# One-column products for carried sums, an ordering edge for node steps, and half runs as row groups in a four-layer graph network

## The chip, the cores and the metric

The kernel runs on one core of a Trainium2 chip. The metric is the device time of one execution in microseconds (us). A core has five engines that run side by side, each with an instruction queue of its own that is worked off in order: TensorE (PE, matrix products; its weight loads are listed as PEld), VectorE (DVE), ScalarE (ACT), GpSimd (POOL, here it issues the indirect transfers) and SyncE (SP, here it issues the plain transfers). TensorE reads SBUF and writes PSUM; the other engines move results on.

## The reference

A residual network of four graph layers over N = 6250 nodes and E = 100000 edges, sorted by destination. Before each layer the node state x (160 columns: 64 scalars, 32 vectors) is normalised and cut at zero to h. A layer mixes h with weights, takes each edge's source row, multiplies it by weights that a small network computes from the edge's features, and adds the edge messages up by node. Layer 3, cut to what matters:

```python
h = jax.nn.silu(edge_scalars @ fc_w1 * (1.0 / np.sqrt(8.0)))
weight = h @ fc_w2 * (1.0 / np.sqrt(64.0))
gs = f_s[edge_src]
gv = f_v[edge_src]
m0a = gs * ys * w1_
m0b = jnp.sum(gv * yv[:, None, :], -1) * INV3 * w4_
m1a = gs[..., None] * yv[:, None, :] * w2_[..., None]
m1b = gv * ys[..., None] * w3_[..., None]
mid = jax.ops.segment_sum(edge_feat, edge_dst, num_segments=N)
```

Layers 0 and 1 have the same form. Layer 2 reads the state at an edge's destination and sums by source:

```python
xs = s[dst]
xv = v[dst]
agg = jax.ops.segment_sum(tp, src, num_segments=N) / DENOM
```

## The kernel before

The edges, sorted by destination, are cut into 56 windows (NW) of 14 tiles (WT) of 128 edges. A window is made of two half runs of 896 consecutive edges; the tiles of the two half runs alternate. A pair of windows is a unit u, and its 28 tiles are worked in 7 groups of G = 4 tiles, so each layer has 28 x 7 = 196 groups.

The program runs in stages. The prologue makes tables of positions and layer 0's node inputs. Then `edges(0)`, `edges(1)`, `messages2`, `sums2` and `edges(3)` follow.

**`edges(li)`**, for layers 0, 1 and 3. Its loop over groups asks for a group's source rows six groups ahead (`gather`: four indirect transfers on POOL, L1277, into `ge`, eight buffers), computes the edge network (`hidden`, L1266 or L1260 with ACT's L1269; `edge_weights`, L1300 or L1293, scaled by ACT into `ws`, L1304 and L1306), and forms the messages on VectorE (`messages`: the selector `oh` L1319, then L1330, L1331, L1333, L1336, L1337, L1338). Four products L1394 add the messages up into `pg`: edges of the first half run land in rows 0 to 63, of the second in rows 64 to 127, each by its node's distance from the first node of its half run.

At a window's end ACT copies `pg` to `acc` (L1397) and a generator `nodes` starts. It takes two steps per group, behind the group's products, in `nodes_out` and `nodes_in`: four products with `turn` (a 0/1 matrix of 128 x 128, L1346) transpose the sums and put the two halves together by node (L1062, into `pt`); ACT copies them to `at` (L1069); VectorE adds the sum of the node that the window before shares with this one: column 0 of that window's `at` to column 1 of this one's (L1073); PE multiplies by the output weights (L1080, L1082); VectorE adds the result to the state `xt` (L1095, L1096, in layer 3 L1115 and on). For layers 0 and 1 the normalisation of the new state and the next layer's node products follow (L991 and on, L999, L1009, L1010, L1022), and SP writes the next layer's `table`, `skip` and `x` (L1034, L1047, L1048). In layers 0 and 1 every third group also takes a step of a generator that sorts the edges by source for layer 2; these are VectorE steps (L1166, L1168, L1171, L1172).

**`messages2`** makes layer 2's messages. For each window SP loads 128 rows of the node table, from the window's first node on (`tb`, L1443), and the destinations of all its 1792 edges, the same to every partition (`dt`, L1445). VectorE compares them with each partition's node (`oh`, L1447). Four products per group (L1479) pick each edge's row, ACT copies the result (L1484 to L1486), VectorE forms the message in `row` (L1497 to L1506, five buffers), and POOL writes each tile's 128 rows to their place by source (L1509).

**`sums2`** reads these rows back in order and sums them on PE (L1611, L1613), with transposes in place of `turn`.

A scheduler in the tile framework orders the instructions on each engine by priority and dependencies. Buffers come from pools; an instruction that reuses one waits for its last reader.

Of the kernel before, what the change touches and what calls it, by code (L numbers as in the profile page):

```python
# [11 lines left out]
F32 = mybir.dt.float32  # L12
# [677 lines left out]
class Fast:  # L690
# [16 lines left out]
    def prologue(self):  # L707
# [119 lines left out]
        nc.tensor.matmul(pw[:, 2, :], lhsT=self.ones[0:1, :], rhs=wd[:, 3, :], start=True, stop=True)  # L827
        nc.vector.tensor_scalar(self.plus_w, pw[:, 0, :], iota_p, None, op0=ALU.add)

        column = pro.tile([P, NW], F32, name="column0")  # L830
        nc.vector.tensor_scalar(column, pw[:, 1, :], place, None, op0=ALU.add)
        other = pro.tile([P, NW], F32, name="other")
        nc.vector.tensor_tensor(other, column, pw[:, 2, :], ALU.not_equal)
# [217 lines left out]
    def nodes_out(self, li, xt, sk, acc, turn, carry, w, wk, pp):  # L1051
# [5 lines left out]
        for k in range(4):  # L1057
            rows, o = (96, 3 * MV) if k == 0 else (MV, (k - 1) * MV)
            if turn is None:
                nc.tensor.transpose(pt[:rows, k, :], acc[:, o : o + rows], self.ident[:n, :n])  # L1060
            else:
                nc.tensor.matmul(pt[:rows, k, :], lhsT=acc[:, o : o + rows], rhs=turn, start=True, stop=True)  # L1062
        yield
# [4 lines left out]
        else:  # L1068
            nc.scalar.copy(at, pt)  # L1069
        if turn is not None:  # L1070

            if carry[0] is not None:
                nc.vector.tensor_add(at[:, :, 1], at[:, :, 1], carry[0][:, :, 0])  # L1073
            carry[0] = at
        yield
# [123 lines left out]

    def at(self, k, most=N):  # L1200

        return self.nc.values_load(self.first[0:1, 2 * k : 2 * k + 1], engines=[mybir.EngineType.SP], min_val=0, max_val=most,
                                   skip_runtime_bounds_check_because="a node's number")

    def edges(self, li):
# [103 lines left out]
        def messages(u, g):  # L1309
# [27 lines left out]
            tt(mvec[:, :, :, 0:64], by3(t1, 64), yv[:, :, :, None].to_broadcast([P, n, 3, 64]), ALU.mult)  # L1337
            tt(mvec[:, :, :, 64:96], e1, by3(ws[:, :, 64:96], 32), ALU.mult)  # L1338
            return oh, msg

        carry = [None]

        def nodes(k, acc):
            xt, sk = xts.pop(k)
            turn = nk.tile([P, P], F32, name="turn")
            nc.vector.tensor_scalar(turn, self.iota, self.column[:, k : k + 1], None, op0=ALU.is_equal)  # L1346
# [35 lines left out]
        for i, (u, g) in enumerate(groups):  # L1382
            prepare(i + AHEAD)
            weights_of(i + 2)
            if i + 1 < len(groups):
                edge_weights(*groups[i + 1])
            oh, msg = messages(u, g)
            for k in range(width(u, g)):
                t = 2 * WT * u + G * g + k
                end = t % WT == WT - 1 or t == TT - 1  # L1390
                if t % WT == 0:
                    pg = p_g.tile([P, AW], F32, name="pg")
                half = slice(HN * (t % 2), HN * (t % 2) + HN)
                nc.tensor.matmul(pg[half], lhsT=oh[:, k, :], rhs=msg[:, k, :AW], start=t % WT < 2, stop=t % WT >= WT - 2)  # L1394
                if end:
                    acc = wk.tile([P, AW], F32, name="acc")
                    nc.scalar.copy(acc, pg)  # L1397
                    live.append(nodes(t // WT, acc))
            data.pop(u - 1, None)
            live = [n for n in live if not (next(n, True) or next(n, True))]  # L1400
            if li < 2 and i % 3 == 0:
# [9 lines left out]
    def messages2(self):  # L1411
# [26 lines left out]
        def select(k):  # L1438

            n = min(WT, TT - WT * k) * P  # L1440
            at = self.at(k)
            tb = ld.tile([P, 160], F32, name="tb")
            nc.sync.dma_start(tb, self.table[2][ds(at, P), :])  # L1443
            dt = ld.tile([P, WT * P], I32, name="dt", bufs=2)
            nc.sync.dma_start(dt[:, :n], self.a["dst_w"][k : k + 1, :n].to_broadcast([P, n]))  # L1445
            oh = ld.tile([P, WT, P], F32, name="oh", bufs=3)
            nc.vector.tensor_scalar(oh.rearrange("p t e -> p (t e)")[:, :n], dt[:, :n], self.plus_w[:, k : k + 1], None,  # L1447
                                    op0=ALU.is_equal)
# [23 lines left out]
        def messages(u, g):  # L1472
            n = width(u, g)
            t0 = 2 * WT * u + G * g
            ts = slice(t0, t0 + n)
            pe = p_e.tile([P, G, 256], F32, name="pe")
            for k in range(n):
                tb, oh = ohs[(t0 + k) // WT]
                nc.tensor.matmul(pe[:, k, :160], lhsT=oh[:, (t0 + k) % WT, :], rhs=tb, start=True, stop=True)  # L1479
            pw = pws.pop((u, g))[:, :n]  # L1480
            pe = pe[:, :n]
            row = wk.tile([P, G, RW], F32, name="row", bufs=5)[:, :n]
            ev = wk.tile([P, G, 224], F32, name="ev", bufs=3)[:, :n]
            nc.scalar.copy(ev[:, :, 0:160], pe[:, :, 0:160])  # L1484
            nc.scalar.copy(ev[:, :, 160:224], pe[:, :, 64:128])
            nc.scalar.copy(row[:, :, 294:390], pe[:, :, 64:160])  # L1486
            nc.scalar.copy(row[:, :, 256:262], self.edge_in[:, ts, :])
# [165 lines left out]
def _layout(inputs):  # L1653
# [46 lines left out]
    a["dst_t"] = by_tile(i["dst"], 1 << 20).T  # L1700
    a["dst_w"] = by_tile(i["dst"], 1 << 20).reshape(NW, WT * P)
    rec0 = np.zeros((E, 8), np.float32)
# [58 lines left out]
```

## Time and profile before

| | us |
|---|---|
| median of three runs | 5459.54 |
| lowest and highest | 5449.31, 5473.62 |
| the profiled execution | 5448.67 |
| its span, first to last instruction | 5446.9 |

The profile is one execution of the program. Its stages, by the first and last indirect transfer of each: prologue to 171 us; layer 0's gathers 171 to 1265; layer 1's 1324 to 2395; layer 2's scatters 2455 to 3550; its sums to 4380; layer 3's gathers 4380 to 5420. A row of the groups reads: line, engine, operation, output and inputs by their names in the program, how many; then the busy time, the mean duration of one in ns, and the idle time of the engine just before them with what ended most of it. Some rows that the change touches:

```profile
L1479 PE MATMUL pe<-tb,oh 128*128 128x160 f32 x1568 | 348.4, 363 | 112.5 <-ACT row L1486 112.3
...
L1062 PE MATMUL pt_out<-turn,acc 128*96 128x128 f32 x1344 | 212.6, 309 | 0.6 <-ACT acc L1397 0.6
...
L1447 DVE TENSOR_SCALAR oh<-dt,plus_w 128x1792 f32<-128x1792 int32 x56 | 65.6, 1171 | 15.8 <-DMA dt<-in_dst_w_dram 15.7
...
L1073 DVE TENSOR_TENSOR at<-at 96x4 f32<-96x4 f32 x165 | 26.7, 162 | 191.6 <-ACT at L1069 190.4
```

A product of f32 operands stands in the trace as two passes: 784 products of L1479 are 1568 rows.

### The profile page before, as it was taken

The numbers are of one execution on the slowest core, as the hardware profiler recorded it, in microseconds if no ns is written. First come the engines' busy times: TensorE is split into PE (matmuls) and PEld (weight loads), VectorE is DVE, ScalarE is ACT, GpSimd is POOL, SyncE is SP. The second block draws the span as 40 slices with busy tenths as digits, with TensorE's granted clock in tenths as the row PEclk, the third lists the DMA queues.
The fourth block names the chain that finished last, engine by engine and source line by source line (L and its number), as shares of the span: only waits on it lengthen the run. The fifth ranks groups of instructions, "written<-read, shape, count | busy, mean of one in ns | idle before, by whom it ended". The sixth has DMA issues, their size and how long they took to land.

```text
span 5446.9 us, 77043 instructions
## 1 busy us (share of the span) xinstructions
PE 4624.0 (85%) x22084; PEld 2866.7 (53%) x22084; DVE 4217.8 (77%) x11655; ACT 2087.1 (38%) x6858; POOL 3346.0 (61%) x3143
## 2 busy tenths in 40 slices
PE   6799999997999999976666666689999988888887
PEld 4455555554555555544444444478888844444443
DVE  6688889888878897867777777767777767777777
ACT  5344444443544444533333333312222243343433
POOL 0577777774777777747777777700000067777776
PEclk9899999998989898987787877799999978788887
DMA  3333333322333333336666666477777533333332
GB/s 95 105 97 88 91 87 90 88 75 73 98 94 94 90 95 93 90 101 239 215 219 215 222 218 223 166 283 237 238 235 237 164 87 80 82 81 82 83 79 57
DMA packets 371211, 733.89 MB, mean 135 GB/s; under 512 B 69677, under 2 KB 249098, under 8 KB 370650
## 3 DMA queue, kind: packets, MB, share of 16 engines
q1 hardware_dynamic: 207122, 379.11, 22.3%
q0 software_dynamic: 163072, 349.43, 22.0%
q8 instruction: 180, 2.95, 0.2%
q14 instruction: 253, 2.07, 0.1%
q10 hardware_dynamic: 584, 0.33, 0.0%
HBM read 519.59 MB, written 209.08 MB: 134 GB/s over the span
## 4 chain that ended last, share of the span: by engine, by line
PE 52%; DVE 16%; DMA 14%; POOL 6%; issue 5%; ACT 3%; SPq 0%; DVEq 0%; ACTq 0%; POOLq 0%
PE pg L1394 12%; PE pg L1613 7%; DMA rec<-row,edge_to 7%; PE pw L1300 7%; DMA ge<-table,rt 6%; PE pg L1611 5%; POOL ge L1277 5%; PE ph L1266 4%; PE pa L1022 3%; PE pt_out L1062 2%; PE po L1082 2%; POOL rec L1509 2%; PE ph L1455 2%; DVE msg L1337 2%; PE pw L1293 2%
## 5 line engine op out<-in xcount | busy, mean ns | idle before, releaser
L1277 POOL DMA_INDIRECT ge<-table,rt x2352 | 2489.1, 1058 | 1774.1 <-DMA skip<-sk 830.3
L1394 PE MATMUL pg<-msg,oh 128*64 128x384 f32 x4704 | 1061.4, 572 | 165.6 <-DVE msg L1338 139.7
L1509 POOL DMA_INDIRECT rec<-row,edge_to x784 | 856.1, 1092 | 299.0 <-issue 191.2
L1304 ACT ACTIVATE ws<-pw,rt 128x96 f32<-128x96 f32 x2352 | 695.8, 348 | 820.5 <-DVE msg L1338 298.6
L1300 PE MATMUL pw<-w_w2y,hh 100*128 100x192 f32 x3136 | 673.5, 353 | 10.6 <-ACT ws L1306 7.7
L1394 PEld LDWEIGHTS pg<-msg,oh 128*64 128x64 f32 x4704 | 305.9, 150 | 709.0 <-issue 252.5
L1300 PEld LDWEIGHTS pw<-w_w2y,hh 100*128 100x128 f32 x3136 | 534.9, 202 | 236.9 <-ACT ws L1306 138.6
L1337 DVE TENSOR_TENSOR msg<-msg,yls 128x768 f32<-128x768 f32 x588 | 555.7, 945 | 0.0
L1613 PE MATMUL pg<-msg,oh 128*120 128x288 f32 x1668 | 541.5, 406 | 0.0
L1330 DVE TENSOR_TENSOR pr<-ge,yls 128x384 f32<-128x384 f32 x588 | 320.2, 545 | 220.7 <-DMA ge<-table,rt 219.9
L1269 ACT ACTIVATE hh<-ph 100x1024 f32<-100x1024 f32 (+1 forms) x336 | 269.1, 801 | 463.7 <-PE pw L1293 206.2
L1479 PE MATMUL pe<-tb,oh 128*128 128x160 f32 x1568 | 348.4, 363 | 112.5 <-ACT row L1486 112.3
L1266 PE MATMUL ph<-ft,w_w1r 12*100 12x512 f32 (+1 forms) x784 | 382.3, 658 | 71.2 <-ACT hh L1269 57.0
L1611 PE MATMUL pg<-rt,oh 128*120 128x192 f32 x1668 | 410.0, 328 | 29.3 <-DMA rt<-rec 29.3
L1479 PEld LDWEIGHTS pe<-tb,oh 128*128 128x128 f32 x1568 | 277.6, 226 | 274.5 <-ACT row L1486 221.9
L1333 DVE TENSOR_TENSOR msg<-ws,ge 128x512 f32<-128x512 f32 x588 | 402.0, 684 | 0.0
L1306 ACT COPY ws<-pw 128x192 f32<-128x192 f32 x1176 | 388.5, 330 | 0.0
L1455 PE MATMUL ph<-ft,w_w1d 128*128 128x512 f32 x224 | 162.4, 819 | 263.2 <-ACT hh L1457 262.4
L1502 DVE TENSOR_TENSOR row<-pw,ev 128x512 f32<-128x512 f32 x196 | 135.2, 690 | 301.8 <-ACT row L1488 298.3
L1611 PEld LDWEIGHTS pg<-rt,oh 128*120 128x120 f32 x1668 | 298.0, 184 | 117.6 <-issue 30.7
L1331 DVE TENSOR_REDUCE dot<-pr 128x128 f32<-128x384 f32 x588 | 344.2, 585 | 0.1
L1338 DVE TENSOR_TENSOR msg<-ge,ws 128x384 f32<-128x384 f32 x588 | 324.4, 552 | 0.0
(486 smaller groups left out, 7327.6 us busy)
## 6 DMA issues: line engine op xcount, KB each, us to landing
rt<-rec SPq DMA_DIRECT2D x208, 780.0 KB
dt<-in_dst_w_dram SPq DMA_DIRECT2D x56, 896.0 KB
ge<-table,rt POOLq DMA_INDIRECT x2352
ft<-in_ft_dram SPq DMA_DIRECT2D x56, 512.0 KB
ft<-in_ft_dram SPq DMA_DIRECT2D x28, 896.0 KB
xt<-x SPq DMA_DIRECT2D x168, 82.0 KB
rec<-row,edge_to POOLq DMA_INDIRECT x784
rt<-in_rec_dram SPq DMA_DIRECT2D x84, 112.0 KB
```

What stands on the lines that cost most here:

```text
L1266: nc.tensor.matmul(ph[:, i], lhsT=w1[r : r + K, :], rhs=ft[r : r + K, 4 * P * (j // 2) :][:, : 4 * P], start=True, stop=True)
L1277: nc.gpsimd.indirect_dma_start(out=ge[:, k, :], out_offset=None, in_=self.table[li], in_offset=bass.IndirectOffsetOnAxis(ap=rt[:, G * g + ...
L1300: nc.tensor.matmul(pw[:, i, :192], lhsT=hh[:, k + i, :], rhs=w2, start=True, stop=True)
L1304: nc.scalar.activation(ws[:, k0 + i, 0:96], pw[:, i, 0:96], AF.Copy, scale=rt[:, G * g + k0 + i, 0:1])
L1306: nc.scalar.copy(ws[:, k0 : k0 + m, 96:192], pw[:, :m, 96:192])
L1333: tt(msg[:, :, AW - 64 : AW + 64].rearrange("p g (k u) -> p g k u", k=2), ws.rearrange("p g (k u) -> p g k u", k=2)[:, :, :, 0:64], e0[:, ...
L1337: tt(mvec[:, :, :, 0:64], by3(t1, 64), yv[:, :, :, None].to_broadcast([P, n, 3, 64]), ALU.mult)
L1394: nc.tensor.matmul(pg[half], lhsT=oh[:, k, :], rhs=msg[:, k, :AW], start=t % WT < 2, stop=t % WT >= WT - 2)
L1479: nc.tensor.matmul(pe[:, k, :160], lhsT=oh[:, (t0 + k) % WT, :], rhs=tb, start=True, stop=True)
L1509: d = nc.gpsimd.indirect_dma_start(out=self.rec2, out_offset=bass.IndirectOffsetOnAxis(ap=self.edge_to[:, t0 + k : t0 + k + 1], axis=0), i ...
L1611: nc.tensor.matmul(pg[:, 0:192], lhsT=oh[:, k, :], rhs=rt[:, k, 0:192], start=first, stop=end, skip_group_check=True)
L1613: nc.tensor.matmul(pg[:, 192:480], lhsT=oh[:, k, :], rhs=msg[:, k, :], start=False, stop=end, skip_group_check=True)
```

## The change

In `nodes_out` VectorE's add of the carried column goes. Instead, behind each of the four products with `turn`, TensorE adds a product with one column: the window before's `acc` times the column 0 of its `turn`, added into column 1 of `pt`. For this `carry` keeps the window before's `acc` and `turn`, and both get four buffers in place of two.

In `edges` the steps of the node generators are traced inside a block that ties VectorE's instructions among them behind the group's last message instruction.

In `messages2` each half run has its own table rows and destinations: partitions 0 to 63 hold the 64 table rows from the first half run's first node on and its 896 destinations, partitions 64 to 127 those of the second. A product contracts the 64 rows of its tile's half run, and the results of the first half run lie in the first bank of `pe`, those of the second in the other; ACT's copies read them in the order of the tiles. `plus_w` and the array `dst_w` are laid out for it.

```diff
-        nc.vector.tensor_scalar(self.plus_w, pw[:, 0, :], iota_p, None, op0=ALU.add)
...
+        nc.vector.scalar_tensor_tensor(self.plus_w, column, -1.0, pw[:, 0, :], op0=ALU.add, op1=ALU.add)
...
-            else:
-                nc.tensor.matmul(pt[:rows, k, :], lhsT=acc[:, o : o + rows], rhs=turn, start=True, stop=True)
+                continue
+            nc.tensor.matmul(pt[:rows, k, :], lhsT=acc[:, o : o + rows], rhs=turn, start=True, stop=carry[0] is None,
+                             skip_group_check=True)
+            if carry[0] is not None:
+
+                sums, turned = carry[0]
+                nc.tensor.matmul(pt[:rows, k, 1:2], lhsT=sums[:, o : o + rows], rhs=turned[:, 0:1], start=False,
+                                 stop=True, skip_group_check=True)
+        if turn is not None:
+            carry[0] = acc, turn
         yield
...
-        if turn is not None:
-
-            if carry[0] is not None:
-                nc.vector.tensor_add(at[:, :, 1], at[:, :, 1], carry[0][:, :, 0])
-            carry[0] = at
...
-            tt(mvec[:, :, :, 64:96], e1, by3(ws[:, :, 64:96], 32), ALU.mult)
-            return oh, msg
+            last = tt(mvec[:, :, :, 64:96], e1, by3(ws[:, :, 64:96], 32), ALU.mult)
+            return oh, msg, last
...
-            turn = nk.tile([P, P], F32, name="turn")
+            turn = nk.tile([P, P], F32, name="turn", bufs=4)
...
-                    acc = wk.tile([P, AW], F32, name="acc")
+                    acc = wk.tile([P, AW], F32, name="acc", bufs=4)
...
-            live = [n for n in live if not (next(n, True) or next(n, True))]
+            with tc.issue_after(last.ins):
+                live = [n for n in live if not (next(n, True) or next(n, True))]
...
-            n = min(WT, TT - WT * k) * P
-            at = self.at(k)
             tb = ld.tile([P, 160], F32, name="tb")
-            nc.sync.dma_start(tb, self.table[2][ds(at, P), :])
-            dt = ld.tile([P, WT * P], I32, name="dt", bufs=2)
-            nc.sync.dma_start(dt[:, :n], self.a["dst_w"][k : k + 1, :n].to_broadcast([P, n]))
-            oh = ld.tile([P, WT, P], F32, name="oh", bufs=3)
-            nc.vector.tensor_scalar(oh.rearrange("p t e -> p (t e)")[:, :n], dt[:, :n], self.plus_w[:, k : k + 1], None,
+            dt = ld.tile([P, WT // 2 * P], I32, name="dt", bufs=2)
+            for h in range(2):
+                rows = slice(HN * h, HN * h + HN)
+                nc.sync.dma_start(tb[rows], self.table[2][ds(self.at(k, half=h), HN), :])
+                nc.sync.dma_start(dt[rows], self.a["dst_w"][2 * k + h : 2 * k + h + 1, :].to_broadcast([HN, WT // 2 * P]))
+            oh = ld.tile([P, WT // 2, P], F32, name="oh", bufs=3)
+            nc.vector.tensor_scalar(oh.rearrange("p t e -> p (t e)"), dt, self.plus_w[:, k : k + 1], None,
                                     op0=ALU.is_equal)
...
-                nc.tensor.matmul(pe[:, k, :160], lhsT=oh[:, (t0 + k) % WT, :], rhs=tb, start=True, stop=True)
+                h, rows = k % 2, slice(HN * (k % 2), HN * (k % 2) + HN)
+                nc.tensor.matmul(pe[:, 2 * h + k // 2, :160], lhsT=oh[rows, (t0 + k) % WT // 2, :], rhs=tb[rows],
+                                 start=True, stop=True)
+            pe = pe.rearrange("p (h t) c -> p t h c", h=2)
+            pair = lambda v: v.rearrange("p (t h) c -> p t h c", h=2)
...
-            nc.scalar.copy(ev[:, :, 0:160], pe[:, :, 0:160])
-            nc.scalar.copy(ev[:, :, 160:224], pe[:, :, 64:128])
-            nc.scalar.copy(row[:, :, 294:390], pe[:, :, 64:160])
+            nc.scalar.copy(pair(ev[:, :, 0:160]), pe[:, :, :, 0:160])
+            nc.scalar.copy(pair(ev[:, :, 160:224]), pe[:, :, :, 64:128])
+            nc.scalar.copy(pair(row[:, :, 294:390]), pe[:, :, :, 64:160])
...
-    a["dst_w"] = by_tile(i["dst"], 1 << 20).reshape(NW, WT * P)
+    a["dst_w"] = np.append(i["dst"], np.full(TT * P - E, 1 << 20, np.int32)).reshape(2 * NW, WT // 2 * P)
```

## The prediction

> **What bounds the kernel now.** I read the page first (engine shares, the 40 slices, the costliest groups), then one table of busy time by stage, then the timeline of POOL, then the waits of each stage, last the chain of waits inside layer 0. The page:
>
> ```profile
> PE 4624.0 (85%) x22084; PEld 2866.7 (53%) x22084; DVE 4217.8 (77%) x11655; ACT 2087.1 (38%) x6858; POOL 3346.0 (61%) x3143
> ...
> POOL 0577777774777777747777777700000067777776
> ...
> L1277 POOL DMA_INDIRECT ge<-table,rt x2352 | 2489.1, 1058 | 1774.1 <-DMA skip<-sk 830.3 <-issue 581.9 <-DVE w_osr L898 170.0
> L1509 POOL DMA_INDIRECT rec<-row,edge_to x784 | 856.1, 1092 | 299.0 <-issue 191.2 <-ACT ev L1485 62.1 <-DVE row L1502 14.6
> ```
>
> POOL looks 61% busy and harmless. But its idle time is a start (170), the stage of layer 2's sums (830), two stage borders (58 and 60), and "issue". The table by stage, in the order layer 0, layer 1, layer 2's messages, its sums, layer 3 (columns: us, busy of PE, PEld, DVE, ACT, POOL, PE clock, DMA share, GB/s):
>
> ```profile
> 171.00:1324.00 1153.00, 1080.18 (x5154) 620.86 (x5154) 1005.81 (x2746) 530.10 (x1650) 855.60 (x785) 0.91 0.34 89
> 1324.00:2455.00 1131.00, 1033.37 (x4768) 568.79 (x4768) 913.09 (x2613) 516.36 (x1732) 832.50 (x785) 0.90 0.36 95
> 2455.00:3550.00 1095.00, 699.30 (x3302) 470.03 (x3302) 778.18 (x1610) 373.32 (x1076) 855.85 (x784) 0.79 0.61 214
> 3550.00:4380.00 830.00, 809.37 (x4292) 680.59 (x4292) 602.45 (x1795) 178.00 (x691) 0.08 (x1) 0.98 0.70 228
> 4380.00:5447.00 1067.00, 890.63 (x4255) 455.67 (x4254) 814.57 (x2403) 406.38 (x1456) 801.20 (x784) 0.83 0.31 79
> ```
>
> The timeline of POOL in layer 2's messages, and VectorE's selector there:
>
> ```profile
> 2824.74 0.97 POOL L1509 DMA_INDIRECT rec<-row,edge_to  x1 [0.30 <-issue]
> ...
> 2826.02 1.68 POOL L1509 DMA_INDIRECT rec<-row,edge_to  x1 [0.30 <-DVE pr L1500]
> ...
> 2826.43 1.15 DVE L1447 TENSOR_SCALAR oh<-dt,plus_w 128x1792 f32<-128x1792 int32 x1
> ...
> 2828.01 1.35 POOL L1509 DMA_INDIRECT rec<-row,edge_to  x1 [0.30 <-issue]
> ```
>
> Every indirect transfer is followed by 0.30 us and the next one, through all four edge stages. 784 of them at the median 0.946 + 0.305 us are 981 us; layers 0, 1 and 3 spend 1094, 1071 and 1040 us from first to last gather, and the rest is transfers that last longer than 0.946. Layer 2's scatters: 784 x (0.972 + 0.305) = 1001 of 1095 us. So POOL, not PE, is what these stages wait for, and no faster compute engine shortens layers 1, 3 or layer 2's messages by itself. VectorE's waits agree (before the first product of a group, for layers 1 and 3):
>
> ```profile
> DVE pr L1330 <- DMA ge<-table,rt: 65.6, 55, 3.7
> ...
> DVE pr L1330 <- DMA ge<-table,rt: 144.1, 70, 6.4
> ```
>
> Layer 0 is different: there that wait is 10.2 us in all, and the last gather is issued at 1265.3 us while the last message ends at 1287.9: the compute side ends some 22 us late (8 us in layer 1: 2394.8 and 2403.2). The chain inside layer 0 (230 to 1262 us):
>
> ```profile
> by line: PE pg L1394 25.5%; PE pw L1300 22.0%; PE ph L1266 13.6%; PE pa L1022 8.6%; PE pt_out L1062 5.0%; ACT hh L1269 3.4%; PE po L1082 2.9%; issue 2.0%; DVE msg L1337 1.7%; PE po L1080 1.3%; POOL ge L1277 1.2%; PE pt_in L1009 1.2%; DVE ms
> ```
>
> Some 80% of it is PE. Layer 0 is the one edge stage where PE is the limit, by a little.
>
> **What the Trainium skill says.** "SBUF — State Buffer", section "SBUF: two separate sides": a transfer issued by GpSimd has its descriptors written by GpSimd's cores, and while VectorE runs an instruction in a two-port mode GpSimd is locked out of SBUF until it ends; an instruction with two SBUF inputs takes the same port. The trace agrees: the two scatters beside L1447 above last 1.68 and 1.35 us instead of 0.97. "TensorEngine Tiling (Array Packing)", "Instruction Overhead": a product with one column costs as much as one with some 60. No run here shows it yet. "TensorE: Matmul & The Clock Gate", "What's actually happening": activity opens the clock, idleness halves it; the table agrees (0.98 in the sums, 0.79 in layer 2's messages), so more PE work will not cost clock, and I put the clock at no change.
>
> **The change part by part.**
> (a) *VectorE's add of the carried column (L1073) goes.* 165 adds x 0.162 = 26.7 us busy, and the 190.4 us that VectorE waited before them for ACT (41.3 in layer 0, 92.4 in layer 1, 56.8 in layer 3). Layers 1 and 3 are POOL's: worth nothing there, the wait moves to the gathers or to the next step, L1095/L1115, which needs the product L1082. In layer 0 some of the 41 comes back, because PE waits for messages.
> (b) *Its replacement on PE:* four one-column products per window, 165 windows with a predecessor, so 660 products; the trace lists each f32 product as two passes, so 1320, and 440 per layer. Price: the existing eight passes of L1062 start at 711.28 and the next product at 712.25, at most 0.12 us each; their 128 columns fill that. A one-column pass is bound by loading 96 weight columns, an estimate of 0.08 us (that TensorE page, "LDWEIGHTS": columns / 1.2). Bounds 0.08 and 0.108, so 35 to 48 us per layer. In layers 1 and 3 it lies beside POOL; PE idles 8% of layer 1 (1033 busy of 1131), so I add 2 us there, up to 15 if that slack can't be used. In layer 0 it stands on the chain: up to +40. Against it stand the 41.3 us under (a), the 9 us that PE idled before L1080 for that add, and what PE waited for messages. I take +8, bounds -18 (the whole lag of 22 us but a rest of 4 goes) and +40.
> (c) *Node steps behind the messages.* In the instruction order of the two built programs VectorE's queue is the same apart from the missing adds: of some 11,000 instructions about 30 change the group they stand in, and PE and ACT shift by a fraction of a group. The new ordering edge pins what stood there already: 0. The third and fourth buffers of acc and turn only keep a window's sums alive for the next: 0.
> (d) *Half runs in layer 2's messages.* The broadcast of destinations shrinks from 128 x 1792 to 2 x 64 x 896 words per window, 917 to 459 KB, 56 times: 51 to 26 MB of the stage's 234 (214 GB/s x 1095 us). Transfers are not what POOL waits for (its waits there are 0.3 us each): 0 in the steady state. The products L1479 contract 64 rows, two of them side by side: PE is 64% busy here, 0. ACT's three copies only read in another order: ACT is busy 373 of 1095 us and waits 482 us for free rows, 0. SP issues four transfers and two register loads per window instead of two and one; 112 more transfers in 1095 us, asked for one window ahead, hidden; if not, the selector would come late, and its slack is a window's 20 us. What counts is L1447: 1.17 to about 0.6 us, 56 times. Over all rows of that stage, 86 of 784 scatters overlap an L1447 and are 0.371 us above 0.97 on average, the other 698 are 0.091 above: 86 x 0.28 = 24 us is its doing. Half as long it meets fewer scatters and holds each a shorter time: a third to a half of the cost is left, a gain of 16 (bounds 8 and 24).
> (e) *Border layer 1 to layer 2:* 60 us, on whose chain the first broadcast (8.8 us) and the write of the last x behind it (12.3 us) stand. With a quarter of the bytes at first, -7 (0 to -13). The prologue swaps one VectorE step for another: 0. The end of layer 3 trades add and wait, about 0.3 us, for eight slow passes: +1.
>
> Sum: +8 +2 -16 -7 +1 = -12 us. The profiled execution took 5448.67 us (span 5446.9), so 5437; the median of the runs shown, 5459.54, is 0.2% above it, and there the sum gives about 5447. I put 5445.
>
> **Rivals.**
> *Faster:* VectorE's waits at nodes were what kept layer 0 behind POOL. Then the lag goes (-18), the selector gives its full 24, the border 10, layer 1 nothing: -50, 5410. For it: in layer 0 VectorE's idle time lies almost wholly at node steps. Against: those waits are for PE, which is late itself.
> *Slower:* the one-column products decide in PE's queue. Layer 0 +40, and layer 1, whose PE load becomes that of layer 0 today, ends 15 us late; less 16 and 7: +32, 5492. It decides from the point where PE's passes per group pass POOL's 5.6 us. For it: pt_out stands on layer 0's chain with all of its time (5.0%; 54 x 0.97 us of these 1032 is 5.1%). Against: PE has idled for the add.
> *The change does nothing on the device's limit:* only the selector counts, -16 to -23 with layer 0 at 0: it is inside the main case.
>
> **How the numbers follow.** Half a per cent (27 us) is about what a measurement of this kernel tells from no change. Main case 45%, own range 5425 to 5465: a third of it is faster by over 0.5%, two thirds within. Faster rival 27%, all faster. Slower rival 28%: 23 slower, 5 within. Sums: faster 0.42, same 0.35, slower 0.23. The range 5392 to 5502 holds both rivals with the spread of the runs (0.2%).
>
> **What would show it.** The gaps of POOL stay 0.30 us in all four stages; the mean scatter falls from 1.092 to about 1.07 us; L1447's successor near 0.6 us; 1320 more passes of 0.08 to 0.11 us; L1073 gone and its wait found before L1095 and the gathers. The lag at layer 0's end tells the rivals apart: 22 us unchanged (main), about 4 (faster), 35 or more with POOL blocked by full buffers (slower). I would be wrong altogether if gathers themselves got shorter or longer in layers 1 and 3, where nothing of this touches them.

## The result and the profile after

The changed kernel takes 5526.66 us (median of 4 runs, 5522.12 to 5552.52), the kernel before in the same series 5466.58 us. The ratio is 1.0126, with a 95% interval of 1.0089 to 1.0163: it is 1.3% slower, and the interval doesn't reach 1. The forecast was 5445, its range ended at 5502. The profiled execution took 5530.79 us (span 5529.0). It lies 82 us above the profiled execution of before, the medians only 60 apart: that execution of before, at 5448.67 us, is among the shortest of its kernel.

The page of the changed kernel, in the lines that answer to those of before:

```profile
PE 4679.0 (85%) x23404; PEld 2969.0 (54%) x23404; DVE 4168.4 (75%) x11490; ACT 2082.5 (38%) x6858; POOL 3299.5 (60%) x3143
...
POOL 0577677775577777773777777720000057777775
...
L1280 POOL DMA_INDIRECT ge<-table,rt x2352 | 2477.0, 1053 | 1880.7 <-DMA skip<-sk 829.8
...
L1517 POOL DMA_INDIRECT rec<-row,edge_to x784 | 821.8, 1048 | 316.7 <-issue 184.0
```

POOL is less busy than before (3299.5 us against 3346.0): its transfers got shorter, the scatters above all (1048 ns on average against 1092). But it sat idle 107 us longer ahead of the gathers (1880.7 against 1774.1). The same five stages by busy time (us, busy of PE, PEld, DVE, ACT, POOL, PE clock, DMA share, GB/s), cut where POOL goes on to the next stage:

```profile
171.00:1413.00 1242.00, 1166.51 (x5594) 693.00 (x5594) 1002.76 (x2697) 532.74 (x1650) 846.52 (x784) 0.88 0.32 83
1413.00:2570.00 1157.00, 1066.23 (x5220) 611.38 (x5220) 902.04 (x2562) 517.39 (x1735) 831.79 (x784) 0.90 0.35 92
2570.00:3630.00 1060.00, 613.75 (x3290) 416.78 (x3290) 752.32 (x1604) 365.24 (x1072) 821.29 (x784) 0.71 0.58 198
3630.00:4460.00 830.00, 808.64 (x4292) 680.40 (x4292) 600.81 (x1791) 176.41 (x690) 0.51 (x1) 0.98 0.70 228
4460.00:5529.00 1069.00, 912.82 (x4695) 496.66 (x4694) 807.30 (x2351) 407.68 (x1457) 798.66 (x784) 0.84 0.31 79
```

Layer 0 takes 1242 us instead of 1153 (+89), layer 1 1157 instead of 1131 (+26), layer 2's messages 1060 instead of 1095 (-35); its sums and layer 3 are as they were. In layers 0 and 1 PE is busy 86 and 33 us longer. What POOL waited for in layer 0 (us in total, times, longest):

```profile
POOL ge L1280 <- issue: 194.8, 639, 0.4
...
POOL ge L1280 <- DVE bst L991: 45.0, 11, 8.8
POOL ge L1280 <- DVE msg L1341: 20.4, 5, 6.8
POOL ge L1280 <- DVE xt L1041: 14.7, 6, 6.0
```

The "issue" row is the 0.30 us between transfers that was there before. The long gaps in the others are new: 32 gaps over 0.35 us, 90 us together. POOL stands until VectorE has done with a gather buffer: 31 of the 32 end 0.27 us after the last read (L1341) of the group eight before, and there are eight buffers. (The rows name whatever VectorE instruction ended nearby.) In the second half of layer 0 of the kernel before, the first VectorE product of a group's messages (L1330) began some 22 us after its last gather. Now it is some 33 us, mostly 30 to 42 (L1333), and there the gather buffers are all taken.

In POOL's own terms this is the whole of layer 0's 89 us: 81 us of gaps beyond 0.30 us each, a border to layer 1 that is 17.5 us longer (75.9 against 58.4), less 9 us of shorter transfers. VectorE's waits in layer 0, before and after:

```profile
DVE at L1073 <- ACT at L1069: 41.3, 24, 3.3
DVE xt L1095 <- PE po L1082: 27.8, 37, 4.8
```

```profile
DVE xt L1098 <- PE po L1085: 130.8, 55, 7.5
DVE xt L1041 <- ACT tb L1033: 67.2, 17, 8.1
DVE hk L1004 <- ACT hn L999: 27.0, 13, 5.7
```

L1098 is the L1095 of before. Its wait for `po` was 27.8 us, with 41.3 us of waiting ahead of the add that is now gone: 69 us have become 131. In layer 1 the same two waits, 116 us together, have become 176.

A stage's length can be split by the clock record of its trace: the time lost to a lowered TensorE clock (length x (1 - granted clock), summed piece by piece), and the rest, the length at full clock. It is an account and not a cause: where a stage doesn't wait for TensorE, a lowered clock need not cost anything (the half runs below are such a case). Each layer with the border behind it, in us, from one execution of each kernel, the experiments below included (A and B mark kernels that ran side by side in one series):

| kernel | layer 0: length | full clock | lost | layer 1: length | full clock | lost |
|---|---|---|---|---|---|---|
| before | 1152.3 | 1052.6 | 99.8 | 1131.0 | 1012.3 | 118.7 |
| changed | 1241.5 | 1089.3 | 152.2 | 1157.1 | 1037.7 | 119.5 |
| one-column products alone (A) | 1229.6 | 1081.0 | 148.6 | 1184.6 | 1041.4 | 143.2 |
| order edge and half runs (A) | 1187.8 | 1056.5 | 131.3 | 1136.9 | 1013.9 | 123.0 |
| changed, update one step later (A) | 1197.2 | 1081.5 | 115.8 | 1152.4 | 1036.1 | 116.3 |
| half runs alone (B) | 1161.6 | 1052.6 | 109.0 | 1133.4 | 1010.3 | 123.1 |
| order edge alone (B) | 1175.3 | 1056.0 | 119.3 | 1136.7 | 1013.7 | 123.0 |
| changed, one-column products twice | 1252.1 | 1135.3 | 116.8 | 1210.9 | 1068.3 | 142.6 |
| half runs, add and update one step later (B) | 1165.5 | 1063.0 | 102.5 | 1123.3 | 1019.3 | 104.0 |

At full clock the passes show plainly: +36.7 us in layer 0 and +25.4 in layer 1 for the change. The other 52.4 us of layer 0 are lost clock, and nearly all of it fell while TensorE was busy (93.3 us lost in busy time before, 145.9 after).

How much clock is lost differs from one execution to the next. But every execution has its span and mean clock on record, so the split can be made for whole kernels over all executions (medians, us):

| kernel | executions | full clock | lost |
|---|---|---|---|
| before (A) | 37 | 4809 | 663 |
| one-column products alone (A) | 4 | 4880 | 695 |
| order edge and half runs (A) | 20 | 4710 | 741 |
| changed, update one step later (A) | 18 | 4764 | 714 |
| changed | 4 | 4759 | 768 |
| changed, one-column products twice | 4 | 4845 | 782 |
| before (B) | 13 | 4812 | 649 |
| order edge alone (B) | 9 | 4818 | 658 |
| half runs alone (B) | 5 | 4689 | 738 |

Rows without a letter are from series of their own. The products alone cost some 70 us at full clock and 32 us of lost clock. (Among the executions of the two kernels the lengths at full clock don't overlap; the lost clock does.) The half runs show why lost clock is no cost by itself: they lose 89 us more of it and are shorter all the same. In the profiled executions 80 us of this lie in layer 2's messages (228.1 before, 308.5 us), where POOL is the limit.

### The profile page after: what moved, and what is told of

Same layout as the page of the kernel before. It is cut to its first block, busy times and chain, and to the rows that moved or that the text cites. A ratio compares the mean times of both kernels' runs of the same rounds, so it can differ in the third digit from the quotient of the medians.

```text
span 5529.0 us, 79941 instructions
## 1 busy us (share of the span) xinstructions
PE 4679.0 (85%) x23404; PEld 2969.0 (54%) x23404; DVE 4168.4 (75%) x11490; ACT 2082.5 (38%) x6858; POOL 3299.5 (60%) x3143
## 4 chain that ended last, share of the span: by engine, by line
PE 25%; DMA 8%; DVE 8%; POOL 6%; issue 4%; ACT 2%; SPq 0%; DVEq 0%; ACTq 0%; POOLq 0%
PE pg L1621 7%; DMA rec<-row,edge_to 6%; PE pg L1619 5%; POOL rec L1517 4%; PE pg L1397 4%; POOL ge L1280 2%; DMA ge<-table,rt 2%; PE pw L1296 2%; PE po L1085 1%; DVE row L1510 1%; PE ph L1263 1%; PE pt_out L1062 1%; PE pa L1022 1%; PE ph L1459 1%; DVE msg L1340 1%
## 5 line engine op out<-in xcount | busy, mean ns | idle before, releaser
L1280 POOL DMA_INDIRECT ge<-table,rt x2352 | 2477.0, 1053 | 1880.7 <-DMA skip<-sk 829.8
L1517 POOL DMA_INDIRECT rec<-row,edge_to x784 | 821.8, 1048 | 316.7 <-issue 184.0
L1303 PE MATMUL pw<-w_w2y,hh 100*128 100x192 f32 x3136 | 686.0, 358 | 13.3 <-ACT ws L1309 10.8
L1333 DVE TENSOR_TENSOR pr<-ge,yls 128x384 f32<-128x384 f32 x588 | 320.8, 546 | 192.0 <-DMA ge<-table,rt 191.3
L1269 PE MATMUL ph<-ft,w_w1r 12*100 12x512 f32 (+1 forms) x784 | 396.2, 674 | 70.9 <-ACT hh L1272 56.8
L1485 PE MATMUL pe<-tb,oh 64*128 64x160 f32 x1568 | 277.4, 410 | 200.2 <-ACT row L1494 198.7
L1485 PEld LDWEIGHTS pe<-tb,oh 64*128 64x128 f32 x1568 | 209.1, 256 | 357.0 <-ACT row L1494 348.1
L1459 PE MATMUL ph<-ft,w_w1d 128*128 128x512 f32 x224 | 182.3, 912 | 218.8 <-ACT hh L1461 218.1
L1341 DVE TENSOR_TENSOR msg<-ge,ws 128x384 f32<-128x384 f32 x588 | 325.3, 553 | 0.0
```

Source lines behind the costliest of these rows:

```text
L1269: nc.tensor.matmul(ph[:, i], lhsT=w1[r : r + K, :], rhs=ft[r : r + K, 4 * P * (j // 2) :][:, : 4 * P], start=True, stop=True)
L1280: nc.gpsimd.indirect_dma_start(out=ge[:, k, :], out_offset=None, in_=self.table[li], in_offset=bass.IndirectOffsetOnAxis(ap=rt[:, G * g + ...
L1303: nc.tensor.matmul(pw[:, i, :192], lhsT=hh[:, k + i, :], rhs=w2, start=True, stop=True)
L1485: nc.tensor.matmul(pe[:, 2 * h + k // 2, :160], lhsT=oh[rows, (t0 + k) % WT // 2, :], rhs=tb[rows], start=True, stop=True)
L1517: d = nc.gpsimd.indirect_dma_start(out=self.rec2, out_offset=bass.IndirectOffsetOnAxis(ap=self.edge_to[:, t0 + k : t0 + k + 1], axis=0), i ...
```

## The experiments

The theories named in the expectations: P, the passes added to PE's queue decide; Q, the order edge decides, since VectorE stands at the node steps behind the messages; W, VectorE's wait for `po` (L1098 behind L1085) is how the passes reach the messages; O, the order edge costs some 36 us in layer 0; V, those 36 us are spread between executions.

In three series the kernel before itself takes 6626 to 6886 us, and there another limit holds (last section): those ratios are listed apart and aren't added to the others.

| kernel | ratio to the kernel before, 95% interval | medians, us | in series with before at 6626 to 6886 us |
|---|---|---|---|
| changed | 1.0126 (1.0089 to 1.0163) | 5526.66 / 5466.58 | |
| one-column products alone | 1.0192 (1.0143 to 1.0241) | 5572.63 / 5473.53 | 1.028 |
| order edge alone | 1.0026 (1.0010 to 1.0043) | 5483.78 / 5468.73 | 1.0018; 1.0016 |
| half runs alone | 0.9938 (0.9918 to 0.9959) | 5426.15 / 5468.73 | 1.0001; 0.9985 |
| order edge and half runs | 0.9960 (0.9947 to 0.9973) | 5452.90 / 5473.53 | 1.0035 |
| changed, update one step later | 1.0024 (1.0008 to 1.0040) | 5484.12 / 5473.53 | |
| changed, products twice | 1.0312 (1.0282 to 1.0343) | 5626.73 / 5461.60 | 1.0561; 1.0629 |
| half runs, add and update one step later | 0.9922 (0.9896 to 0.9947) | 5415.50 / 5468.73 | 1.0068 |

The three parts alone sum to +1.9 +0.3 -0.6 = +1.6%, the whole is +1.3%: they add up within the intervals.

**The one-column products alone.** The kernel before with this in place of L1073 (and `turn` and `acc` in four buffers):

```diff
+                nc.tensor.matmul(pt[:rows, k, 1:2], lhsT=sums[:, o : o + rows], rhs=turned[:, 0:1], start=False,
+                                 stop=True, skip_group_check=True)
...
-                nc.vector.tensor_add(at[:, :, 1], at[:, :, 1], carry[0][:, :, 0])
```

> The kernel before with the one-column products alone in place of VectorE's add (turn and acc in four buffers with them). Theory P (TensorE's queue: the added passes decide in layers 0 and 1): +115 us on the kernel before: layer 0 ends its gathers near 1337 us instead of 1265, POOL waits some 90 us in it for buffers, both stage borders are 17 us longer, layer 1 is 8 us longer, layer 2's messages are unchanged at 1095 us. Theory Q (VectorE stands at the node steps behind the messages and waits for products there, so the order edge decides): below +30 us, layer 0's gathers end before 1290 us.

> The one-column products alone, once more, because in the first four runs the kernel before itself took 6640 us, with gaps on ScalarE that nothing in the program explains, and POOL no longer set the pace of any stage. Where the kernel before takes about 5460 us, theory P (added passes) expects +115 us with layer 2's messages at 1095 us; theory Q (order edge and wait) below +30 us. Where it takes 6640 us again: +2.8% as in the first run.

It takes 99 us more than the kernel before, with layer 2's messages at 1094 us: P, and not Q. POOL's long gaps in layer 0 are 77 us, where P had 90. In layer 1 P was too low: its gathers take 32 us longer instead of 8, with 37 us of such gaps. The windows of layers 0 and 1 of this kernel:

```profile
171.00:1402.00 1231.00, 1158.90 (x5594) 685.82 (x5594) 1001.25 (x2687) 532.52 (x1650) 843.89 (x785) 0.88 0.32 83
1402.00:2586.00 1184.00, 1096.46 (x5208) 628.54 (x5208) 902.76 (x2559) 516.77 (x1732) 831.53 (x785) 0.88 0.35 91
```

The loss is in these two: 77 and 54 us in the profiled execution, at a clock of 0.88 instead of 0.91 and 0.90. What the products cost by themselves is seen in one window's block, before and in the changed kernel (start, length, what, and at the end of a row how many passes):

```profile
711.28 1.04 PE L1062 MATMUL pt_out<-turn,acc 128*96 128x128 f32 x8
712.25 0.71 PE L1022 MATMUL pa<-w_asn,ht 64*128 64x128 f32 x4
```

```profile
1072.87 0.46 PE L1062 MATMUL pt_out<-turn,acc 128*96 128x128 f32 x2
1073.17 0.25 PE L1067 MATMUL pt_out<-turn,acc 128*96 128x1 f32 x2
1073.28 0.44 PE L1062 MATMUL pt_out<-turn,acc 128*96 128x128 f32 x2
...
1074.45 0.90 PE L1303 MATMUL pw<-w_w2y,hh 100*128 100x192 f32 x4
```

From its first pass to the next product the median block of layer 0 lasts 1.57 us, against 0.97 us before: 0.60 us for 8 passes, 0.075 us each. Those are blocks at full clock. 11 of the 56 in the changed kernel's layer 0 ran at half clock, and there the block takes 2.97 us against 1.83, so a pass costs 0.14 us. The mean duration of a row of L1067 overstates this (209 ns a pass in layer 0), because neighbouring rows overlap. At full clock 55 windows make some 33 us a layer.

**The changed kernel without the one-column products**, that is the order edge and the half runs with VectorE's add kept:

```diff
-                nc.tensor.matmul(pt[:rows, k, 1:2], lhsT=sums[:, o : o + rows], rhs=turned[:, 0:1], start=False,
-                                 stop=True, skip_group_check=True)
...
+                nc.vector.tensor_add(at[:, :, 1], at[:, :, 1], carry[0][:, :, 0])
```

> The changed kernel with VectorE's add of the carried column in place of the one-column products. Theory P: -35 us on the kernel before, the same as the half runs alone. Theory Q: +60 - 35 = +25 us or more, POOL waits in layer 0.

> The changed kernel with VectorE's add in place of the one-column products, once more. Where the kernel before takes about 5460 us: theory P expects -35 us, all of it in layer 2's messages, and layer 0's last gather at 1265 us; theory Q +25 us or more.

`turn` and `acc` are back in two buffers as well. This kernel takes 20.6 us less than the kernel before. The one-column products, with the buffers that they need, are the whole of the loss and more; the buffers weren't tried without the products. P's -35 was too much: layer 0 with its border is 1187.8 us here.

**The half runs alone, and the order edge alone.**

> The kernel before with only layer 2's messages in half runs. Theory P and the selector's part: -35 us (layer 2's messages from 1095 to about 1060 us, mean scatter from 1.092 to 1.048 us), both borders near 58 to 60 us. If the gain in that stage came from what the products changed around it and not from the half runs: within 10 us of the kernel before.

> The half runs alone, where POOL sets the pace (the kernel before near 5460 us). With VectorE's add kept and the order edge both, the time was 20.6 us below the kernel before, 38 us less in layer 2's messages and some 18 us more in layer 0 and 18 at its border. If the order edge costs these 36 us (theory O), the half runs alone give -40 to -55 us and layer 0 with its border takes 1152 us as before. If layer 0 varies by that much from run to run (theory V), they give -20 us, like both together.

> The half runs alone, where the kernel before takes about 5460 us. Theory O (the order edge cost 36 us in layer 0 and its border): -40 to -55 us. Theory V (layer 0 varies by that much by itself): about -20 us, as with the edge. Where the kernel before takes over 6500 us: within 0.3% of it, as twice before.

> The kernel before with only the node steps pinned behind the groups' messages. Theory P: within 0.3% of the kernel before (16 us), gathers of layer 0 end at 1265 us as before. Theory Q: +60 us or more, POOL waits for buffers in layer 0.

> The order edge alone, where POOL sets the pace. Theory O: +20 to +36 us, layer 0 with its border some 36 us above 1152 us, by a lower TensorE clock there (some 131 us of clock lost as against 100). Theory V: within 8 us of the kernel before.

> The order edge alone, where the kernel before takes about 5460 us. Theory O: +20 to +36 us, with more TensorE clock lost in layer 0 than 100 us. Theory V: within 8 us of the kernel before.

The half runs alone take 42.6 us less than the kernel before, as O had it. The order edge alone takes 15.1 us more, between O and V, and far from Q's 60. Layer 2's scatters, of the half runs alone, and the selector there:

```profile
L1513 POOL DMA_INDIRECT rec<-row,edge_to x784 | 815.6, 1040 | 296.7 <-issue 180.0
```
```profile
L1447 DVE TENSOR_SCALAR oh<-dt,plus_w x55: 674/685/904, 2469.1 to 3454.3; 128x896 f32<-128x896 int32 x55
```

The stage takes 1054.0 us instead of 1095.2, all of it shorter scatters (815.6 us against 856.1); the gaps are 0.30 us as before. Over all rows of the stage the 86 scatters that overlap a selector are 0.099 us above 0.97, where they were 0.371, and the other 698 are 0.067 above, where they were 0.091. So 21 of the 24 us laid to the selector are gone, and 17 us more come from scatters that no selector touches. Why those got shorter isn't settled; that 24 MB less move in this stage (210 instead of 234) is one candidate, and it wasn't tried alone.

The order edge shows in layer 0: 1175.3 us with the border, against 1161.6 for the half runs alone in the same series, with the lag of the last message behind the last gather at 30 instead of 23 us. From first to last gather, layer 0 of the half runs alone is to 0.1 us as long as that of the kernel before (1094.0 and 1093.9 us, 87.0 us of lost clock in both). Its border is 9 us longer (67.6 against 58.4), though nothing of the half runs touches it, so differences of that size between single executions are spread. The 14 us fit O's direction and not its size. The two kernels with the edge and VectorE's add lost 131.3 and 119.3 us of clock in a layer 0 whose code is the same, and over all executions the edge alone loses 8 us more than the kernel before.

**The changed kernel with VectorE's update one step further back.** The generator of a window pauses once more between the products and the update:

```diff
         pv = po[:, v0:].rearrange("p (c w) -> p w c", c=3)
         yield
+        if turn is not None:
+            yield
```

> The changed kernel with one more step between the products po and VectorE's update that reads them, so that the update stands one group further back. In the changed kernel VectorE waits 130.8 us for po in layer 0. If that wait is how the added passes reach the messages (theory W), layer 0 gives back at least half of its 72 us. If the passes themselves fill TensorE (theory P), layer 0 gives back less than 15 us.

VectorE's waits in its layer 0, and the layer's window:

```profile
DVE xt L1041 <- ACT tb L1033: 104.2, 47, 9.4
DVE hk L1004 <- ACT hn L999: 55.6, 27, 4.7
DVE xt L1100 <- PE po L1085: 18.7, 15, 5.3
```
```profile
171.00:1369.00 1198.00, 1126.24 (x5594) 664.73 (x5594) 1005.45 (x2699) 528.50 (x1650) 842.22 (x785) 0.90 0.33 86
```

The wait for `po` falls from 130.8 to 18.7 us; 66 us of it come back at the next node steps. From first to last gather layer 0 gives back 49 of its 72 us (44 of 89 with the border), with every added pass still there (5594 passes), and the kernel is 0.24% above the kernel before instead of 1.26%. This is W's outcome. The gain stands in the lost clock: in layer 0 the length at full clock falls by 8 us only, the lost clock by 36, and over all executions of the whole kernel the first rises by some 5 us and the second falls by 54. Why the clock is better there isn't shown. Layer 3's gathers take 11 us more (1048.6 against 1037.2 us), but those of kernels without the later step there lie between 1032 and 1050, so nothing can be laid to the step.

**The one-column products issued twice.**

```diff
+                for last in (False, True):
+                    nc.tensor.matmul(pt[:rows, k, 1:2], lhsT=sums[:, o : o + rows], rhs=turned[:, 0:1], start=False,
+                                     stop=last, skip_group_check=True)
```

> The changed kernel with every one-column product issued twice, so that the carried sums enter twice (the result is another one for that). Theory P (time goes with the passes): layer 0 has 37 us more of TensorE work at full clock per 440 passes, so about +40 to +60 us there, and layer 1, which is now at its balance, +30 to +60 us: +70 to +120 us on the changed kernel, +130 to +180 us on the kernel before. Theory W (VectorE's wait for po decides, passes count only as its delay): each window's po comes 0.6 us later, 110 windows: +66 us at most in layers 0 and 1 and TensorE's clock falls below 0.88 there; layer 3 the same as before in both.

> The changed kernel with every one-column product issued twice (the carried sums enter twice), where the kernel before takes about 5460 us. The block of one window measured 0.61 us longer for its 8 one-column passes, so the second set is 33 us of TensorE work in each of layers 0, 1 and 3. Theory P (layers 0 and 1 are now full, time goes with the passes alone): layer 0 with its border +33 to +40 us and layer 1 with its border +33 to +40 us on the changed kernel, layer 3 within 5 us: +65 to +80 us in all. Theory W (each pass also delays po and with it VectorE and the messages, as half of the first 89 us did): +75 us or more in layer 0 with its border alone, over +120 us in all.

> As before this, where the kernel before takes about 5460 us: theory P, layers 0 and 1 with their borders +33 to +40 us each on the changed kernel and layer 3 within 5 us, +65 to +80 us in all; theory W, over +75 us in layer 0 with its border alone, over +120 us in all.

By the medians' ratios it is 1.8% above the changed kernel (101 us), between the two theories as the last two expectations put them, and inside P's wider range in the first. The profiled execution was the shortest of its four (5579.05 us, the median is 5626.73) and stands 48 us above the changed kernel's:

```profile
171.00:1423.00 1252.00, 1182.39 (x6034) 715.38 (x6034) 1003.11 (x2697) 530.49 (x1650) 842.30 (x784) 0.91 0.31 82
1423.00:2634.00 1211.00, 1132.52 (x5652) 666.36 (x5652) 900.30 (x2557) 517.85 (x1733) 820.11 (x784) 0.88 0.33 88
```

Layer 0 is only 11 us longer, layer 1 54 us: neither P's 33 to 40 in each nor W's 75 in layer 0. The median block of layer 0 grew by 0.68 us this time. At full clock the layers grew by 46 and 31 us, near what the second set of passes is long (some 37 us). The lost clock fell by 35 us in layer 0 and rose by 23 in layer 1. This execution lost unusually little, 708 us in all where the median is 782. Over all executions the second set costs some 86 us at full clock and 14 us of lost clock. So in this account the passes cost about their own length in both layers, once these have nothing left to hide them, and the lost clock on top is no fixed price per pass.

**The half runs, with the add and the update each one step further back in layers 0 and 1**, without order edge and one-column products:

```diff
+            if li < 2:
+                yield
             if carry[0] is not None:
                 nc.vector.tensor_add(at[:, :, 1], at[:, :, 1], carry[0][:, :, 0])
...
         yield
+        if turn is not None and li < 2:
+            yield
```

> The half runs with VectorE's add, without order edge or one-column products, and in layers 0 and 1 with the add one step behind ScalarE's copy and the update one step behind po, so that VectorE waits for neither. Theory W: VectorE's 69 us of waits in layer 0 (41.3 for the copy, 27.8 for po) go, TensorE's lag at its end falls from 22 to below 10 us, and the time is 12 to 25 us below the half runs alone. Theory P: no TensorE work is saved, so it equals the half runs alone within 8 us.

> The half runs with VectorE's add and update each one step further back in layers 0 and 1, where the kernel before takes about 5460 us. Theory W: 12 to 25 us below the half runs alone, lag of layer 0's end below 10 us. Theory P: within 8 us of the half runs alone. It was 0.8% above them where the kernel before took 6886 us.

It takes 5415.50 us, the shortest of all: 0.78% below the kernel before and 2% below the changed one. The step from the half runs alone, 10.7 us, is inside the intervals of both. And it isn't where W put it: layer 0's lag is 34 us, not below 10 (last message 1293.6 us, last gather 1259.1), and VectorE waits 81.9 us for the copy ahead of the add. Its waits at node steps in layer 0 sum to 134 us, where the half runs alone have 138: they moved and didn't go. Layer 1 has the gain. Its window for the half runs alone and for this kernel:

```profile
1333.00:2466.00 1133.00, 1036.34 (x4772) 568.97 (x4772) 911.90 (x2615) 517.24 (x1733) 836.65 (x784) 0.89 0.35 93
```
```profile
1337.00:2460.00 1123.00, 1022.86 (x4776) 567.04 (x4776) 905.96 (x2609) 519.12 (x1734) 825.02 (x784) 0.91 0.36 95
```

POOL's transfers there are 12 us shorter in sum (825.0 against 836.7). Other VectorE instructions stand beside them now; that this is why wasn't tried.

## Why the prediction was wrong, step by step

**What bounds the kernel.** POOL was read rightly as the limit of layers 1, 3 and layer 2's messages, and layer 0 as the one stage where PE is. But "POOL is the limit" was taken as cover. PE was busy 1033 of 1131 us in layer 1 and 1080 of 1153 in layer 0. Such a stage has two limits close together, and an engine at 91 to 94% gave no cover for some 35 us more. In layer 3, where PE was busy 891 of 1067 us, the same number of passes cost nothing that shows: 1069 us with them.

**(a) and (b), the step that failed.** The price of a pass was about right: 0.075 us at full clock against bounds of 0.08 to 0.108, though 0.14 at half clock. Wrong is what was set against it: layer 0 was put at +8 (bounds -18 to +40) by crediting VectorE's removed waits, and came to +89 with its border in the profiled pair. The 69 us of waits didn't go; they moved to `po` and became 131. Nor had PE idled 9 us for the add: the rows that name L1073 before L1080 in layer 0 sum to 5. Here a wait wasn't saved by removing the waiting instruction, because the next one reads what the same chain makes a little later. Layer 1 was put at +2 (to +15) and came to +26, of which 18 are the longer border. Without the credit the sum for layer 0 would have been +40, still 49 short, which is about what the next term left out.

**The clock.** "More PE work will not cost clock" was costed at nothing without a bound. In the profiled pair 52.4 us of layer 0's 89 are lost clock; over all executions the products alone lose 32 of their 99 us to it. The Trainium skill, "TensorE: Matmul & The Clock Gate", section "What's actually happening", says that activity opens the clock and idleness halves it. The traces agree as far as the values go: their clock records hold 1.0 and 0.5 and nothing else. I read only the page's first half into the forecast: the passes bring work, but also waits. This case's traces don't give a fixed price: layer 0 with its border lost 99.8 us before, 148.6 and 152.2 with the products, 115.8 with the update moved and 116.8 with the products doubled. Some of it is the draw of one execution. What sets it stays open.

**(c) Order edge, costed at 0:** +15 us (0.26%, interval 0.10 to 0.43%). Of VectorE's 11,000 instructions the whole change moves about 30 to another group, and layer 0, where the edge shows, has little slack; by which of these steps it costs wasn't traced.

**(d) Half runs, costed at 16 (8 to 24):** 41 us in the stage, 42.6 in the whole (35 in the stage for the changed kernel). The mechanism held: the scatters beside the selector, L1451 in the changed kernel, which takes 0.69 us instead of 1.16. The term was too small twice: nearly all of the selector's 24 us went, not a third to a half, and the other scatters gave 17 more. The Trainium skill, "SBUF — State Buffer", section "SBUF: two separate sides", says that VectorE locks GpSimd out of SBUF while it runs an instruction in a two-port mode. The fall from 0.371 to 0.099 us agrees with that; whether the selector runs in such a mode no trace here shows.

**(e) Borders and tail:** layer 1 to layer 2 by -7: the half runs alone show -1.7 (59.9 to 58.2 us). In the changed kernel it is 78.2 us, where layer 1 ends with a lag of 25 instead of 8 us. The tail was put at +1 and is 4.3 longer.

**The rivals.** The slower one named the mechanism, and its mark was there: POOL blocked by full buffers in layer 0. It was priced at 5492, 35 us short: it had the passes' own length in layer 0 (+40) and a late end of layer 1 (+15), but neither the lost clock nor layer 0's longer border. Its chance, 28%, was too small beside a main case that rested on a credit. The faster rival, that VectorE's waits held layer 0 behind POOL, failed because the waits didn't go. Whether layer 0 would be shorter without them stays untested: no kernel here got rid of them, and with the add and the update pushed back the half runs' last message comes at 1293.6 us instead of 1288.0.

**Marks.** POOL's gaps stayed 0.30 us in layer 2's messages and layer 3, not in layer 0 (90 us in longer ones) and layer 1 (11 us). The lag at layer 0's end is 30 us, between the 22 of the main case and the 35 of the slower rival. The mean scatter fell further than foretold, to 1.048 us. VectorE's wait went to the update that reads `po`, as foretold, but grew. 1320 passes came, near the price foretold. The gathers' own time in layers 1 and 3, the mark of being wrong altogether, stayed within 3 us.

## What to carry to other kernels

When one engine is busy for nearly all of a stage that another also fills (here TensorE for 91 and 94% of it), a few per cent more work for it isn't hidden; in the stage where it was busy 83% it was. Ask what is free in that stage for exactly the time added, and put the stage's longer border on the bill. Removing an instruction that waits saves only its busy time, if the engine's next instruction needs the end of the same chain; putting the reader a step further back can win some of the wait, as the run with the later update shows in layer 0. And hold a single profiled execution against all the others on record before building on its numbers. And of a change with several parts each is worth a run alone: here one part of three is good, and alone it beats the whole by some 100 us.

## What the runs showed of the hardware that was not expected

In three series the kernel before took 6626, 6642 and 6886 us, 21 to 26% more, with ScalarE's and VectorE's instructions as long as elsewhere (L1304 348 ns in both, L1337 943 ns against 945). ScalarE stops there for nothing that the program explains. Of the run with the order edge in the series at 6642 us (start, length, wait before it):

```profile
711.87 0.35 ACT L1306 COPY ws<-pw 128x192 f32<-128x192 f32 x1
717.97 0.48 ACT L1397 COPY acc<-pg 128x384 f32<-128x384 f32 x1 [5.76 <-remote]
```

Waits of ScalarE with no releaser in the program sum to 1280 us in that run and to 20 us in the kernel before where it takes 5449 us. TensorE's products and VectorE have such waits too (374 and 446 us, against 0 and 3). POOL no longer sets the pace in any of the four edge stages: it idles 142 to 388 us in each in gaps over 0.35 us, where it had about 1 us at most. There the half runs gain nothing to 0.15%, and each set of 1320 passes costs about 3%. What stops the engines is open. The fetches of instructions that the trace lists aren't longer there (medians of 0.99 and 0.40 us on their two queues, against 1.03 and 0.38). Whether the device decides isn't shown: the record gives the number 12 to the device of a series at 5469 us and of the next one at 6626 us, and whether that is one device or two isn't known.
